# A graph-attention stack on one core: the end of the last block in another order, and another choice of score slots behind it

## The chip, the cores and the metric

The kernel runs on one core of one Trainium2 chip. The metric is the device time of one execution in microseconds (us), lower being better; the median of three runs is given. Profiles show one further execution, with the start and duration of every instruction on the core's engines: PE (matrix products), DVE and ACT (elementwise work on two engines of different instruction sets), POOL (a slower elementwise engine) and SP (which here only issues transfers). Each engine takes its instructions in the order in which they stand in its own queue.

## The reference

The input is `x` of shape (16, 1024, 128) and one 0/1 matrix `adj` of shape (1024, 1024). Three transformer layers with masked attention (8 heads of 16) are followed by one graph-attention layer:

```python
# layers 0, 1, 2
Q, K, V = (h @ Wq, h @ Wk, h @ Wv)            # split in 8 heads of 16
scores = einsum('bnhd,bmhd->bhnm', Q, K) / sqrt(16)
attn = softmax(where(adj == 0, -inf, scores))
x = layer_norm(h + (attn @ V) @ Wo + bo)
x = layer_norm(x + relu(x @ W1 + b1) @ W2 + b2)
# layer 3
h = x @ W;  s_i = h @ a_src;  s_j = h @ a_dst
e = leaky_relu(s_i[:, :, None] + s_j[:, None, :], 0.2)
att = nan_to_num(softmax(where(adj == 0, -inf, e)))
out = layer_norm(att @ h + x)
```

All is float32.

## The kernel before, in words

The work of a layer of one batch is a *block*: 48 blocks, m = 0 to 47, from 3 layers times 16 batches. Batches go in groups of four, so the last four blocks, 44 to 47, are layer 2 of the batches 12, 13, 14 and 15. A block has 32 *steps*, one for each of two groups of four heads, two halves of 512 queries and eight tiles of 128 keys. A step (`score_step`) makes four 128x512 tiles of exponentials (one for each head): PE writes scores into one of three PSUM *score slots* of 1,024 float32 (tag `s`, `slot()`), DVE or POOL puts the mask on, ACT takes the exponential. In five steps of eight ACT reads the scores first and POOL multiplies by the 0/1 mask (`L430`, about 2.15 us); the rest is masked by an addition on DVE (`L432`). Four steps later (`AHEAD`) `av_step` multiplies the exponentials by the values into one accumulator (`L449`). When the eight steps of a half are done, `finish` takes the accumulator out.

All other work is cut into *pieces*, small functions that put their instructions into the queues when called. There are chains of pieces:

- `proj_tasks`: the eight pieces of the next block's projections;
- `post_tasks`: for blocks 0 to 46 the eleven pieces behind a block's attention (gather, two of the output projection, two transposes, four of the first and two of the second feed-forward product); for block 47 the same work in two chains of six, one for each half of the queries (*final* 0 and 1), where half 0 can begin after step 19;
- `last_tasks`: for a batch whose layer 2 is done, the twelve pieces of layer 3, called the *last chain* below: two transposes (`xt`), three of `nodes`, `rows_gh`, then `edges(0)`, `edges(1)` with `aggregate(0)`, `edges(2)` with `aggregate(1)`, `edges(3)` with `aggregate(2)`, `aggregate(3)` and `end`. `rows_gh` turns columns into rows and issues 16 small transfers; `edges` (`L606`, `L609`) makes masked weights through two score slots, `aggregate` (`L296`, 128 matrix products) multiplies by them, and `end` normalises and stores.

The order is a plan made before anything runs. `now` counts steps. A piece is due at a fixed step of the block where the table `AT` names its chain (`proj` and `post`), or else so many steps after the piece before it in its chain. Behind each step `piece()` calls one due piece, of the first chain in the list that has one. In the block after a block of batch b, `AT["post"]` puts the last two pieces of `post_tasks(b)`, the two halves of the second feed-forward product, at steps 32 and 40, which is step 0 and step 8 of the block after that. The chain `last` follows in the same queue, its first piece five steps later.

After step 31 of block 47 come eight more turns (`for n in range(n, n + 2 * AHEAD)`), in which the last four `av_step`s and one piece each are called, and then the loop `while chains`, which goes on counting and calls every due piece of every chain. I call the time from the end of the last `av_step` on the *tail*.

PE and ACT get their instructions in the order of this plan (`tc.manual_schedule`). The order on DVE, POOL and SP is the framework's, which builds it from the same program. Pieces write their matrix products into `bank()`: one PSUM bank of 512 float32 with a single buffer (tag `t`), except at the head of the program (`head[0]`), where it is half of a score slot. A piece that needs the bank waits until the piece before has been read out of it.

The changed lines are in `bank`, `rows_gh`, `put`, `av_due` and the end of the plan's loop. In `rows_gh` four pairs of transfers for r = 0 go to SP; the four pairs for r = 1 go to the ACT queue for the batches 14 and 15, to SP otherwise.

Of the kernel before, what the change touches and what calls it, by code (L numbers as in the profile page):

```python
# [31 lines left out]


AT = {"proj": (3, 6, 9, 11, 14, 15, 19, 20), "post": (12, 22, 23, 25, 26, 27, 28, 30, 32, 40, 41)}
AHEAD = 4
BOTH_ON_DVE = (2, 5, 7)
TILES = {"w": 10, "x": LANES + 1, "last": 2}
# [77 lines left out]
def fast_path(ctx: ExitStack, tc: tile.TileContext, a: dict, out: bass.AP, flag):  # L115
    nc = tc.nc
    x_dram, adj = a["x"], a["adj"]
    B, N, D = x_dram.shape
    NT = N // P
# [9 lines left out]
    def slot(dtype=F32):  # L129

        return psum.tile([P, N], dtype, tag="s", name="s", bufs=3)

    def bank():

        if head[0]:
            return slot()[:, :512]
        return psum.tile([P, 512], F32, tag="t", name="t", bufs=1)

    head = [True]

    def half_tile(name):

# [81 lines left out]
    def first_weights():  # L224
        W[0].update(load_layer(nc, nc.sync, const, a, 0, ("Wo", "b2", "W1", "b1", "W2", "ln1_g", "ln2_g")))
        norm_weights(nc.sync, 0)
# [49 lines left out]
    def soon():  # L276

        return nullcontext() if head[0] else tc.high_priority(offset=SOON)
# [167 lines left out]
    def av_step(step, e, acc, first, last):  # L446
        m, g, qh, kt = step
        for j in range(J):
            nc.tensor.matmul(acc[j * SLOT:j * SLOT + HD + 1, :], v_bufs[m % 2][:, kt, 2 * j + g, :], e[:, j, :],  # L449
                             start=first, stop=last)  # L450
# [89 lines left out]
    def last_tasks(b):  # L540
# [39 lines left out]
        def rows_gh():  # L580
            ps = bank()[:2 * NT, :P]
            nc.tensor.transpose(ps, s["col"][:, 0:2, :].rearrange("p c t -> p (c t)"), identf)
            parts = work.tile([2 * NT, 2, P], F32R, tag="parts", name="parts", bufs=1)
            with soon():
                nc.scalar.copy(parts[:, 0, :], ps)
                nc.vector.tensor_sub(parts[:, 1, :], ps, parts[:, 0, :].bitcast(F32))  # L586
            for r in range(2):

                queue = nc.scalar if r and b >= B - 2 else nc.sync
                for i in range(4):  # L590
                    row = 64 * r + g0 + i
                    queue.dma_start(g_rows[row:row + 1, :].bitcast(F32), parts[:NT, i // 2, :].bitcast(F32))
                    queue.dma_start(h_rows[row:row + 1, :].bitcast(F32),
                                    parts[NT + 4 * r:NT + 4 * r + 4, i % 2, :].bitcast(F32))
# [59 lines left out]
    blocks = [(b, l) for p in range(0, B, LANES) for l in range(L) for b in range(p, p + LANES)]  # L654
    chains = []
    done = {("fetch", b) for b in range(2)}
    now = [0]
    free = dict(TILES)
    free["x"] -= 2

    def put(tasks, mark, chain=None, first=False):

        if chain is None:
            chain = {"due": now[0], "queue": deque()}
            chains.insert(0 if first else len(chains), chain)
        for n, task in enumerate(tasks):
            at = now[0] // (4 * NT) * 4 * NT + AT[mark[0]][n] if mark[0] in AT else None
            chain["queue"].append(task + (mark if n == len(tasks) - 1 else None, at))
        return chain

    def take(chain):

        _, f, tiles, mark, _ = chain["queue"][0]
        if any(free[t[1:]] == 0 for t in tiles.split() if t[0] == "+"):
            return False
        chain["queue"].popleft()
        f()
        for t in tiles.split():
            free[t[1:]] += -1 if t[0] == "+" else 1
        done.add(mark)  # L680
        chain["due"] = now[0]
        if not chain["queue"]:
            chains.remove(chain)
        return True

    def is_due(chain):
        gap, at = chain["queue"][0][0], chain["queue"][0][4]
        return now[0] >= (chain["due"] + gap if at is None else at)

    def piece():  # L690
        for chain in chains:
            if is_due(chain) and take(chain):
                return

    def need(mark):
        while mark not in done:
            first = next(c for c in chains if any(q[3] == mark for q in c["queue"]))
            assert take(first) or any(take(c) for c in list(chains) if c is not first)
# [27 lines left out]
    def av_due(n):  # L726

        for item in [w for w in waiting if w[2] <= n]:
            step, e, _ = item
            half = step[:3]  # L730
            if half not in accs:
                if accs:
                    continue
                accs[half] = sums
                left[half] = NT
            waiting.remove(item)
            left[half] -= 1
            av_step(step, e, accs[half], left[half] == NT - 1, left[half] == 0)
            if left[half]:
                continue  # L740
            m, g, qh = half
            b, l = blocks[m]
            while g == 0 and qh == 0 and last_attn:
                need(last_attn.pop())
            finish(g, qh, accs.pop(half))()
            if m == len(blocks) - 1:
                if g == G - 1:
                    if qh == 0:
                        final.append(post_tasks(b, l)[1])
                    put(final[0][qh], ("final", qh), first=True)  # L750
                    if qh == 1:
                        put(last_tasks(b), ("last", b), chains[0])
            elif g == G - 1 and qh == 1:
                post = post_tasks(b, l)[0]
                chain = put(post[:1], ("attn", b, l))
                put(post[1:], ("post", b, l), chain)
                last_attn.append(("attn", b, l))
                if l == L - 1:
                    put(last_tasks(b), ("last", b), chain)

    n = 0
    with tc.manual_schedule(engines={mybir.EngineType.PE, mybir.EngineType.Activation}):
        for m, (b, l) in enumerate(blocks):
            order = [(g, qh) for g in range(G) for qh in range(2)]
            if m in (0, len(blocks) - 1):
                order.sort(key=lambda x: x[1])
            for at, (g, qh, kt) in enumerate((g, qh, kt) for g, qh in order for kt in range(NT)):
                now[0] = n
                if at == (6 if m == 0 else 1):
                    stack(m, 1)  # L770
                if n == 6:
                    with tc.issue_after(behind["stack"]):
                        first_weights()
                        other_weights()
                if n == 20:
                    with tc.issue_after(behind["pool"]):
                        biases()
                if n == 40:
                    with tc.issue_after(behind["dve"]):
                        last_weights()  # L780
                if at == 0 and m + 2 < len(blocks) and blocks[m + 2][1] == 0:
                    put([(0, fetch(blocks[m + 2][0]), "+x")], ("fetch", blocks[m + 2][0]))
                if m + 1 < len(blocks):
                    if at == (6 if m == 0 else 0):
                        need(("post",) + (blocks[m + 1][0], blocks[m + 1][1] - 1) if blocks[m + 1][1] else
                             ("fetch", blocks[m + 1][0]))
                        put(proj_tasks(m + 1), ("proj", m + 1), first=True)
                    if at == (24 if m == 0 else 21):
                        need(("proj", m + 1))
                        stack(m + 1, 0)  # L790
                step = m, g, qh, kt
                if FIRST <= n < FIRST + 4:

                    with tc.manual_schedule(engines={mybir.EngineType.DVE}):
                        e = score_step(step)
                        neighbours(4 + n - FIRST)
                        masks(4 + n - FIRST, mask_rows(4 + n - FIRST))
                else:
                    e = score_step(step)
                waiting.append((step, e, n + AHEAD))  # L800
                av_due(n)
                piece()
                n += 1
        exponentials(0)
        for n in range(n, n + 2 * AHEAD):
            now[0] = n
            av_due(n)
            piece()
        while chains:
            now[0] += 1  # L810
            for chain in list(chains):
                if is_due(chain):
                    take(chain)
# [236 lines left out]
```

## Time and profile before

| | us |
|---|---|
| median of 3 runs | 4011.02 (4008.79 to 4011.72) |
| the profiled execution, span from first to last instruction | 4007.5 |
| block 45, step 0 to step 0 of the next (steps 3623.2 to 3696.4) | 73.2 |
| block 46 (3696.4 to 3773.0) | 76.6 |
| block 47 (3773.0 to 3874.2) | 101.2 |
| the last four `av_step`s (to 3884.3) | 10.1 |
| tail to the end of the span | 123.2 |
| PE busy, of the whole span | 3767.4 (94%) |
| DVE, ACT, POOL busy | 85%, 84%, 86% |

The starts of the blocks are those of their first score products (`L422`, four to a step). Times inside the span are us from its start. A row of the table of stretches gives the stretch, its length and the busy time of each engine in it with the number of instructions. `PEclk` is the share of its full clock that PE was granted. In the list of instructions the bracket at the end of a row is the time in which the engine stood idle before it, and what ended that.

### The profile page before, as it was taken

The page shows a single profiled execution, that of the slowest core. Times are in us where ns is not written, and L with a number is a line of the kernel's source. Part 1 is how long each engine was busy: PE and PEld are TensorE (multiplying, and loading weights), DVE is VectorE, ACT ScalarE, POOL GpSimd, SP SyncE. Part 2 cuts the span into 40 slices and gives each one's busy share as a digit, 9 for nine tenths or more (in the row PEclk, how much of TensorE's full clock was granted, in tenths as well). Part 3 has the DMA queues.
Part 4 walks back from the last instruction along what each step waited for, and adds up shares of the span by engine and source line. Part 5 has one row for each costly group of instructions (what it writes and reads, how often), then busy time and mean ns, then how long its engine had stood idle before and what let it go on. Part 6 is the DMA issues. An engine that isn't in the chain of part 4 may idle for free.

```text
span 4007.5 us, 107755 instructions
## 1 busy us (share of the span) xinstructions
PE 3767.4 (94%) x44501; PEld 1551.0 (39%) x44501; DVE 3412.3 (85%) x5326; ACT 3380.2 (84%) x3961; POOL 3450.1 (86%) x3010
## 2 busy tenths in 40 slices
PE   7999999999999999999999999999999999999986
PEld 2333333344443333334444333333444433333435
DVE  7888988988888988988888988988888898988864
ACT  7999999977779999997777999999777799999850
POOL 5889989988889989998788999989888899989884
PEclk8999999999999999999999999999999999999998
DMA  6222122212222222122222222222222121222100
GB/s 162 64 65 59 49 64 65 53 46 67 55 56 59 56 64 64 48 60 55 55 55 55 64 64 57 51 64 65 55 55 55 49 64 49 59 65 62 46 7 20
DMA packets 124465, 233.13 MB, mean 58 GB/s; under 512 B 34624, under 2 KB 73792, under 8 KB 123968
## 3 DMA queue, kind: packets, MB, share of 16 engines
q1 hardware_dynamic: 122960, 225.71, 22.5%
q8 instruction: 354, 5.80, 0.6%
q14 instruction: 143, 1.17, 0.1%
q10 hardware_dynamic: 1008, 0.44, 0.0%
HBM read 15.54 MB, written 8.39 MB: 6 GB/s over the span
## 4 chain that ended last, share of the span: by engine, by line
PE 60%; DVE 17%; POOL 16%; issue 4%; ACT 3%; SPq 1%; DMA 0%; ACTq 0%; DVEq 0%; POOLq 0%
PE acc L449 23%; PE t L296 19%; PE s L422 15%; DVE e L432 10%; POOL e L430 7%; POOL x L344 3%; POOL x L345 3%; DVE st L321 3%; PE t L285 2%; POOL mv L338 1%; DVE x L328 1%; ACT e L444 1%; DVE lo L385 1%; DVE mv L323 1%; POOL x L340 1%
## 5 line engine op out<-in xcount | busy, mean ns | idle before, releaser
L432 DVE TENSOR_TENSOR e<-s,mask_add 128x1024 f32<-128x1024 f32 x2112 | 2492.6, 1213 | 315.1 <-PE s L422 206.5
L444 ACT ACTIVATE e<-e 128x1024 f32<-128x1024 f32 x2112 | 2193.6, 1062 | 197.5 <-DVE e L432 181.6
L430 POOL TENSOR_TENSOR e<-e,mask 128x1024 f32<-128x1024 f32 x960 | 2052.9, 2152 | 343.4 <-ACT e L429 326.9
L449 PE MATMUL acc<-e,v 128*17 128x512 f32 x12288 | 1636.2, 604 | 61.9 <-POOL e L430 30.4
L422 PE MATMUL s<-Wq,Wk 64*128 64x512 f32 x6144 | 1177.0, 455 | 50.1 <-DVE e L432 33.6
L429 ACT ACTIVATE e<-s 128x1024 f32<-128x1024 f32 x960 | 982.9, 1024 | 245.9 <-PE s L422 245.8
L422 PEld LDWEIGHTS s<-Wq,Wk 64*128 64x128 f32 x6144 | 499.3, 186 | 1011.1 <-issue 397.5
L449 PEld LDWEIGHTS acc<-e,v 128*17 128x17 f32 x12288 | 208.0, 95 | 574.1 <-issue 466.9
L340 POOL TENSOR_SCALAR x<-x,mv 128x128 f32<-128x128 f32 x896 | 389.1, 448 | 23.5
L296 PE MATMUL t<-hd,e 128*32 128x129 f32 x8192 | 243.5, 276 | 5.7 <-DVE x L624 3.3
L338 POOL TENSOR_TENSOR mv<-mv,half_neg 128x4 f32<-128x4 f32 x224 | 232.5, 1038 | 18.6
L344 POOL TENSOR_TENSOR x<-x,ln_g 128x1024 f32<-128x1024 f32 (+1 forms) x97 | 229.6, 2367 | 10.3 <-PE t L285 6.3
L296 PEld LDWEIGHTS t<-hd,e 128*32 128x32 f32 x8192 | 226.3, 111 | 23.9 <-DVE lo L385 9.9
L328 DVE TENSOR_TENSOR x<-t,x 128x512 f32<-128x512 f32 x192 | 131.5, 685 | 93.5 <-PE t L296 93.5
L296 PE MATMUL t<-x1T,W 128*32 128x512 f32 x1536 | 200.1, 592 | 1.9 <-DVE x L624 1.0
L321 DVE BATCH_NORM_STATS2 st<-x 128x6 f32<-128x128 f32 x896 | 197.0, 279 | 3.3
L296 PEld LDWEIGHTS t<-W,hT 128*32 128x32 f32 x6144 | 174.0, 111 | 59.9 <-issue 45.5
L296 PE MATMUL t<-W,hT 128*32 128x128 f32 x6144 | 188.1, 275 | 1.8 <-ACT x1T L290 0.9
L285 PEld LDWEIGHTS t<-identf,x 128*128 128x128 f32 x888 | 95.8, 142 | 227.6 <-issue 87.5
L285 PE MATMUL t<-identf,x 128*128 128x128 f32 x888 | 156.0, 291 | 27.0 <-DVE parts L586 7.4
L385 DVE TENSOR_TENSOR lo<-t,hi 128x512 fp32r<-128x512 f32 x188 | 128.2, 682 | 35.6 <-ACT hi L384 35.6
L336 POOL TENSOR_SCALAR mv<-mv 128x4 f32<-128x4 f32 x224 | 53.0, 236 | 122.6 <-DVE mv L323 102.7
(97 smaller groups left out, 2507.7 us busy)
## 6 DMA issues: line engine op xcount, KB each, us to landing
Wk<-hi SPq DMA_DIRECT2D x384, 128.0 KB
Wk<-lo SPq DMA_DIRECT2D x384, 128.0 KB
Wq<-hi SPq DMA_DIRECT2D x384, 128.0 KB
Wq<-lo SPq DMA_DIRECT2D x384, 128.0 KB
x<-in_x_dram SPq DMA_DIRECT2D x16, 512.0 KB
out_dram<-x SPq DMA_DIRECT2D x31, 256.0 KB
ai<-in_adj_dram SPq DMA_DIRECT2D x8, 512.0 KB
g_rows<-parts SPq DMA_DIRECT2D x120, 4.0 KB
```

What stands on the lines that cost most here:

```text
L285: nc.tensor.transpose(ps[:, t * P:(t + 1) * P], src[:, 4 * h + t, :], identf)
L296: nc.tensor.matmul(dst[j:j + SLOT, :], lhsT[:, j:j + SLOT], rhs, start=start, stop=stop)
L321: nc.vector.bn_stats(st[:, t, :], z[:, t, :])
L338: nc.gpsimd.tensor_tensor(v, v, half_neg[:, ts], OP.pow)
L340: nc.gpsimd.tensor_scalar(z[:, t, :], z[:, t, :], mv[:, t, 0:1], mv[:, t, 1:2], op0=OP.add, op1=OP.mult)
L344: nc.gpsimd.tensor_mul(z, z, rows(gain, n))
L422: nc.tensor.matmul(ps[:, r * 512:(r + 1) * 512], k[64 * r:64 * r + 64, kt * P:(kt + 1) * P], q[64 * r:64 * r + 64, q0:q0 + 512], start=Tru ...
L429: nc.scalar.activation(ev, psv, AF.Exp, scale=HD ** -0.5)
L430: behind["pool"] = nc.gpsimd.tensor_mul(ev, ev, m).ins
L432: behind["dve"] = nc.vector.tensor_add(ev, psv, m).ins
L444: nc.scalar.activation(ev, ev, AF.Exp, scale=HD ** -0.5)
L449: nc.tensor.matmul(acc[j * SLOT:j * SLOT + HD + 1, :], v_bufs[m % 2][:, kt, 2 * j + g, :], e[:, j, :], start=first, stop=last)
```

## The change

The change does four things, all at the end of the program.

1. A second table, `AT_END`, gives other due steps to the ten timed `post` pieces of blocks 45 and 46 (`len(blocks) - m` is 3 and 2). For block 45 (batch 13) the two second feed-forward pieces are due at steps 30 and 31 of block 46. For block 46 (batch 14) all ten are due at steps 8 to 21 of block 47.
2. Since a `last` chain follows its `post` chain in the same queue, the last chains of batches 13 and 14 begin earlier too.
3. A flag `tail` is set where the loop `while chains` begins; from there on `bank()` is half of the next score slot, as at the head of the program, so all pieces and `edges` take the three slots in turn.
4. The r = 1 transfers of batch 14's `rows_gh` go to SP; only batch 15 keeps half of them on the ACT queue.

```diff
+AT_END = {3: (12, 21, 22, 24, 25, 26, 27, 28, 30, 31), 2: (8, 9, 13, 14, 15, 16, 17, 18, 20, 21)}
...
-        if head[0]:
+        if head[0] or tail[0]:
             return slot()[:, :512]
         return psum.tile([P, 512], F32, tag="t", name="t", bufs=1)
 
-    head = [True]
+    head, tail = [True], [False]
...
-                queue = nc.scalar if r and b >= B - 2 else nc.sync
+                queue = nc.scalar if r and b == B - 1 else nc.sync
...
-    def put(tasks, mark, chain=None, first=False):
+    def put(tasks, mark, chain=None, first=False, table=None):
...
-            at = now[0] // (4 * NT) * 4 * NT + AT[mark[0]][n] if mark[0] in AT else None
+            at = now[0] // (4 * NT) * 4 * NT + (table or AT[mark[0]])[n] if mark[0] in AT else None
...
-                put(post[1:], ("post", b, l), chain)
+                put(post[1:], ("post", b, l), chain, table=AT_END.get(len(blocks) - m))
...
+        tail[0] = True
         while chains:
```

## The prediction

> **What bounds the kernel now.** I read the stretches of time first, cut at the end of block 47's steps, the last product with the values (3884.3, which I call E), the first `edges` of batch 14 (3953.4) and the last aggregate.
>
> ```profile
> 3773.00:3874.20 101.20, 90.19 (x1307) 43.53 (x1303) 81.17 (x152) 65.00 (x79) 79.21 (x83) 0.93 0.11 28
> 3884.30:3953.40 69.10, 44.74 (x944) 34.47 (x941) 27.11 (x87) 8.38 (x26) 37.01 (x53) 0.79 0.04 11
> 3953.40:3995.10 41.70, 38.33 (x1093) 34.17 (x1089) 28.18 (x69) 0.65 (x4) 17.42 (x27) 0.93 0.06 17
> 3995.10:4007.50 12.40, 0.19 (x2) 0.11 (x2) 2.22 (x15) 0.00 (x0) 5.76 (x9) 0.70 0.17 49
> ```
>
> The first number after the length is PE. In block 47 it is busy 90.2 of 101.2 us, so a piece moved there is mostly paid there. In the first 69.1 us of the tail it is busy 44.7, partly at half clock: this stretch is waiting. Then come eight aggregates, bound by PE, and 12.4 us of closing work that the change leaves alone.
>
> The list of instructions tells who is waited for.
>
> ```profile
> 3839.43 8.39 POOL L430 TENSOR_TENSOR e<-e,mask 128x1024 f32<-128x1024 f32 x4
> 3841.62 1.91 PE L449 MATMUL acc<-e,v 128*17 128x512 f32 x8 [4.20 <-POOL e L430]
> 3849.20 1.30 PE L296 MATMUL t<-Wo,aT 128*32 128x128 f32 x32 [2.68 <-DVE aT L476]
> ...
> 3944.37 0.78 ACT L290 ACTIVATE xT<-t,ln_bc,ln_gc 128x512 f32<-128x512 f32 x1 [6.32 <-DMA g_rows<-parts]
> 3945.29 1.09 PE L285 MATMUL t<-identf,x 128*128 128x128 f32 x4 [5.94 <-ACT xT L290]
> ...
> 3967.36 3.75 PE L296 MATMUL t<-hd,e 128*32 128x129 f32 x128 [0.36 <-DVE x L624]
> 3991.30 3.75 PE L296 MATMUL t<-hd,e 128*32 128x129 f32 x128 [1.02 <-DVE x L624]
> ```
>
> In block 47 PE twice stands for POOL: four mask products are queued behind normalisations (4.20 us), and POOL's last step of a `finish` holds the next projection (2.68). In the tail ACT issues eight row transfers of batch 14 before it may evict batch 15's transpose, and PE stands 5.94 us. An aggregate is 3.75 us; the gap before it is 1.02, of which an `edges` (0.74) fills most where there is one.
>
> The chain that ended last shows the same: POOL until 3848, then PE and POOL in turn, ACT's queue at 3938 to 3944, then aggregates.
>
> ```profile
> 3839.48 8.34 POOL e L430 x4
> 3938.09 1.25 ACTq L592
> 3944.37 0.79 ACT xT L290
> 3956.32 5.20 PE t L296 x128
> 3962.58 3.79 PE t L296 x128
> ```
>
> **What the Trainium skill says.** "TensorE: Matmul & The Clock Gate", Part 1: an idle window of about 3.4 us puts PE at half clock until it has been busy for as long. The trace agrees: behind the 4.20 us wait a value product takes 1.91 us, not 1.05, and behind the 5.94 us wait an aggregate takes 5.21, not 3.75. "Perfetto Trace Analysis", Per-engine timelines: ACT, DVE and GpSimd are strict first-in first-out, PE pulls only weight loads ahead. The three waits above are such heads of queues. "Trainium Kernel Development and Optimization", Key Constraints: issuing transfers from several engines saves only issue time. In the trace that is much: batch 13's 16 transfers on SP take 3875.66 to 3886.37, 10.7 us, batch 15's 8 on SP beside 8 on ACT 6.2 (3955.25 to 3961.4).
>
> **Where the pieces go.** By the plan's rules with both tables, and by the queues of the two programs: from the tail (or the turns before it) to ahead of E come three `edges` and two aggregates of batch 13 and the two second feed-forward pieces of batch 14. Four first feed-forward pieces of batch 14 were ahead of E already. Left in the tail: half 1 of block 47, two aggregates of batch 13, and the last chains of 14 and 15. So the change does what it says. Batch 13's chain only gets half of its way, though.
>
> **Part 1: E.** PE work that comes in ahead of it: 3 x 0.74 + 2 x 3.75 + 2 x 1.93 = 13.6 us. What could hide it is the idle time of block 47, 11.0 us, of which the two POOL waits make 6.9 and half clock costs about 3.8 more. Does POOL's queue come out better? I set its new order against the PE pieces, with the durations of the trace: mask product 2.15, normalisation 3.3 (0.24 + 0.23 + 1.04 + 1.74 and small gaps), scale and shift 2.6 per half, 4.8 per whole. The old pile, a normalisation and 7.4 us of scaling ahead of four masks, is broken up. But the second normalisation behind batch 14's output projection now stands behind batch 12's last normalisation and scaling (5.9) and two masks (4.3), while its transpose is on PE already at step 19: the projection ends 52 us into the block, plus 2 for DVE; POOL reaches it at 61 and ends at 64.3; PE wants it at 59.6, so it stands 4.7 us. Two steps later the projection of half 0 waits about 2 us, as before, for a `finish` behind a mask product, and a transpose of the final chain 0.9. That is 7.6 where it was 6.9. I take no gain and E 13.6 later: about 3898. Bounds: 4 later if the stalls vanish (13.6 less 6.9 and most of the half clock), 19 if a new stall adds 5.
>
> **Part 2: E to batch 14's edges.** In before 69.1 us. In after, us from E, each from rows of before's tail:
> - the projection of half 1 starts at 2.7 (0.7 + 0.3 + 0.6 + 0.7 for transpose, reciprocal, POOL, transpose, and hand-overs) and ends at 3.8; DVE adds, and masks one half of batch 13's `edges(3)` first (1.2) before the statistics, to 7.0;
> - POOL meanwhile has batch 13's normalisation and scaling (5.9, from 1.9 to 7.8), then half 1's to 11.1;
> - transpose and ACT to 12.0, feed-forward 13.1, aggregate 3 of batch 13 16.9, feed-forward 17.9, nodes 18.8, second feed-forward 20.8, two more nodes 22.3, transpose and `rows_gh` 23.3, cast and difference 24.8;
> - SP has the second store of batch 13 ahead of these transfers: aggregate 3 (16.9) + DVE 2.0 + POOL 3.3 + 2.6, so 24.8 too. Transfers start at about 25.2;
> - all 16 on one queue: 10.7, and at most 1.7 until they can be used (batch 13: 3886.37 to 3888.06): 37.6. I add 1.5 for half clock in the chain: 39.
>
> PE is through batch 15's nodes at about 31 and waits for the transfers, with batch 15's `rows_gh` behind it. With half on ACT it would have been about 5 us less, but ACT would have been held. Saving: 69.1 - 39 = 30.1. Bounds: 37 if no half clock, 45 if half clock falls on the whole chain.
>
> **Part 3: aggregates.** In before 41.7, of which half clock is 1.5 (first aggregate) and about 1.2 (`edges`). Slots in turn do little: two for an `edges` and one for an aggregate is a period of three, so an aggregate gets the slot of the one before and waits as it did. The turn is broken where two `edges` follow one another: aggregate 2 of batch 14 gets the slot that batch 15's first mask pass reads, and waits for it, about 3.0 us more. Twice an aggregate follows another with no `edges` between; it takes another slot and saves 1.0. Net +1.0, the half clock kept: 42.7. Bounds 39 and 48. The closing 12.4 stays.
>
> The sum: 39 + 42.7 + 12.4 = 94.1 against 123.2, 29.1 less; E 13.6 later; net -15.5. The span goes from 4007.5 to 3992; the median of the runs stands 3.5 above the profiled span, so I forecast 4011.0 - 15.5 = 3995.5, say 3995. What a measurement can tell from no change is about 0.2%, 8 us: 4003 to 4019.
>
> **Rivals.**
> - *The likeliest*, paid in the block and earned twice over in the tail: 3995, own range 3987 to 4004. For it: PE idle 24 us in the first part of the tail. Chance 0.60, of which 0.05 lies within 0.2%.
> - *The block hides the work*: POOL's pile gone, no half clock, E only 4 later: 3986, down to 3979. For it: 11 us idle there. Against: POOL is as loaded as PE (79 + 5 us). Chance 0.21.
> - *The transfers take the gain*: SP is still on batch 13's store when rows are ready, 16 transfers in line, PE cold behind: batch 14's edges at 50 and not 39, aggregates 46; -15.5 + 11 + 3 gives 4009.5, no change. Against: the store's chain ends at 24.8 by the sum. Chance 0.11 (0.02 faster, 0.08 same, 0.01 slower).
> - *Slower*: the slots in turn bind. If each aggregate waited for the mask passes in its slot (2.4 us on DVE) as well as its own eviction, the eight aggregates cost 19 more; from -15.5 that is +3.5, 4014; with E 19 late instead of 13.6, 4020. It decides from 23.5 us over my sum, all eight aggregates with E at its late bound. Against: the slot order makes one pay. Chance 0.08.
>
> So faster 0.55 + 0.21 + 0.02 = 0.78, same 0.05 + 0.08 = 0.13, slower 0.09. The range 3979 to 4009 takes in the second rival and most of the third.
>
> **What would show it.** E near 3898 (3888 to 3904), block 47 some 107 us; a PE wait of 4 to 5 us before a transpose (`L286`) two thirds through it; 16 row transfers in a line on SP about 25 us behind E, and PE idle some 6 us before the `edges` that follow; one aggregate with a gap of 3 to 4 us before it, the others 1.0. I am wrong if E hardly moves, if the transfers aren't what batch 14's edges wait for, or if aggregates are more than 5.5 us apart.

## The result, and the profile after

The changed kernel takes 3994.27 us (median of 4 runs, 3992.41 to 3997.75), beside 4011.37 us for the kernel before on the same chip. The ratio is 0.9958, with a 95% interval of 0.9946 to 0.997: 17 us faster. The profiled execution has a span of 3990.6 us, where before it was 4007.5.

First the stretches of time of the changed kernel, cut at the same events as before: block 47's steps, the last four value products, E to the first `edges` of batch 14, the aggregates, the closing. Columns: stretch, length, busy time of PE, PEld, DVE, ACT and POOL with the number of instructions, granted clock, DMA share, GB/s.

```profile
3773.90:3876.70 102.80, 91.14 (x1289) 43.42 (x1285) 82.38 (x154) 67.90 (x83) 86.19 (x90) 0.97 0.09 25
3876.70:3894.20 17.50, 17.33 (x444) 12.40 (x440) 12.67 (x35) 3.87 (x5) 7.90 (x15) 1.00 0.01 3
3894.20:3933.50 39.30, 24.96 (x529) 20.01 (x527) 14.36 (x55) 7.65 (x28) 30.93 (x40) 0.79 0.06 17
3933.50:3978.20 44.70, 40.21 (x1088) 36.08 (x1088) 27.83 (x68) 0.26 (x1) 16.33 (x27) 0.88 0.06 16
3978.20:3990.60 12.40, 0.22 (x5) 0.11 (x2) 2.22 (x15) 0.00 (x0) 6.86 (x10) 0.65 0.17 49
```

The moved work is hardly seen in block 47, which is only 1.6 us longer than before, but in the line after it: the last value products take 17.5 us instead of 10.1, and PE is busy in 17.33 of them. (Block 46, which takes in one second feed-forward piece of batch 13, is 1.8 us longer.) E moves to 3894.2. From E to batch 14's edges there are 39.3 us where there were 69.1. The aggregates take 3 us more, the closing is the same.

The list of instructions of the changed kernel shows the waits; the bracket is the idle time before an instruction and what ended it.

```profile
3841.19 1.77 PE L286 MATMUL t<-identf,x 128*128 128x128 f32 x4 [4.58 <-POOL x L341]
3849.00 1.08 PE L297 MATMUL t<-Wo,aT 128*32 128x128 f32 x32 [1.56 <-DVE aT L477]
3897.06 1.93 PE L297 MATMUL t<-Wo,aT 128*32 128x128 f32 x32 [2.84 <-DVE aT L477]
3902.51 19.04 SPq L639 DMA_DIRECT2D out_dram<-x  x2
3923.50 1.77 PE L286 MATMUL s<-identf,x 128*128 128x128 f32 x4 [4.52 <-POOL x L341]
3933.53 1.19 PE L607 MATMUL s<-g_rows,h_rows 4*128 4x256 f32 x7 [4.97 <-DMA h_rows<-parts]
3944.06 3.75 PE L297 MATMUL s<-hd,e 128*32 128x129 f32 x128 [0.45 <-DVE x L625]
3951.52 5.28 PE L297 MATMUL s<-hd,e 128*32 128x129 f32 x128 [0.69 <-DVE e L610]
```

In block 47 the two waits for POOL of before (4.20 and 2.68 us) have become one of 4.58 at another place, the transpose of batch 14, and one of 1.56. In the tail PE no longer stands for ACT, but for the input of half 1's projection (2.84), for POOL (4.52) and for the row transfers (4.97). The last two lines are aggregates 1 and 2 of batch 14: 3.7 us lie between the end of the one and the start of the other, where others with an `edges` between them are 1.0 to 1.1 apart.

The chain that ended last, of the changed kernel (start, length, engine and what it works on):

```profile
3841.19 1.79 PE t L286 x4
...
3919.88 1.27 POOL x L346
3921.17 0.38 SPq L639
3921.64 0.65 SPq L593
...
3931.73 1.67 DMA h_rows<-parts
...
3937.53 5.46 PE s L297 x128
```

It runs through POOL's last operation on batch 13's output into the store of that output on SP, from there through the 16 row transfers of batch 14 in one line, and then into the aggregates.

### The profile page after: what moved, and what is told of

Read it like the earlier page. It is cut to its first block, busy times and chain, and to the rows that moved or that the text cites. A ratio compares the mean times of both kernels' runs of the same rounds, so it can differ in the third digit from the quotient of the medians.

```text
span 3990.6 us, 107765 instructions
## 1 busy us (share of the span) xinstructions
PE 3758.4 (94%) x44501; PEld 1550.6 (39%) x44501; DVE 3410.8 (85%) x5326; ACT 3380.6 (85%) x3961; POOL 3454.8 (87%) x3010
## 4 chain that ended last, share of the span: by engine, by line
PE 60%; DVE 18%; POOL 14%; issue 4%; ACT 3%; SPq 0%; DMA 0%; DVEq 0%; POOLq 0%; ACTq 0%
PE acc L450 23%; PE t L297 18%; PE s L423 15%; DVE e L433 10%; POOL e L431 7%; POOL x L345 3%; POOL x L346 3%; DVE st L322 3%; PE t L286 2%; DVE x L329 1%; POOL mv L339 1%; ACT e L445 1%; DVE lo L386 1%; PE s L297 1%; DVE mv L324 1%
## 5 line engine op out<-in xcount | busy, mean ns | idle before, releaser
L341 POOL TENSOR_SCALAR x<-x,mv 128x128 f32<-128x128 f32 x896 | 392.0, 453 | 23.5
L345 POOL TENSOR_TENSOR x<-x,ln_g 128x1024 f32<-128x1024 f32 (+1 forms) x97 | 230.0, 2372 | 11.7 <-PE t L286 6.1
L297 PE MATMUL t<-hd,e 128*32 128x129 f32 x7040 | 207.8, 275 | 1.2
L297 PEld LDWEIGHTS t<-hd,e 128*32 128x32 f32 x7040 | 193.5, 110 | 16.7 <-DVE lo L386 9.9
L610 DVE SCALAR_TENSOR_TENSOR e<-s,mask 128x1024 f32<-128x1024 f32 x128 | 150.3, 1213 | 6.1 <-PE s L607 5.4
```

What stands on the lines that cost most here:

```text
L297: nc.tensor.matmul(dst[j:j + SLOT, :], lhsT[:, j:j + SLOT], rhs, start=start, stop=stop)
L341: nc.gpsimd.tensor_scalar(z[:, t, :], z[:, t, :], mv[:, t, 0:1], mv[:, t, 1:2], op0=OP.add, op1=OP.mult)
L345: nc.gpsimd.tensor_mul(z, z, rows(gain, n))
```

## The experiments

Blocks ahead of the change differ by up to 9 us from profile to profile (block 46 begins at 3692.8 to 3701.6), so I count every profile from the first score product of block 46. *E* is then the length from there to E; the next columns are the stretches behind it. A profile is one execution, and the runs of one kernel scatter by some 5 us either way (28 runs of before on one chip: 4005.7 to 4016.06): where the time lies is read from the profile, the worth of a kernel from the ratio. The ratio is to runs of the kernel before on the same chip. e1 to e4, e5 to e8 and e9 to e12 ran on three different chips, with medians for before of 4011.19, 4009.13 and 4011.16 us, so medians of different groups are compared only roughly.

| kernel | flag | table | row queue of batch 14 | E | E to edges | aggregates | closing | sum | median us | ratio to before |
|---|---|---|---|---|---|---|---|---|---|---|
| before | | | ACT+SP | 187.9 | 69.1 | 41.6 | 12.5 | 311.1 | 4009.13 to 4011.37 | 1 |
| the change | x | x | SP | 198.7 | 39.3 | 44.7 | 12.4 | 295.1 | 3994.27 | 0.9958 (0.9946 to 0.997) |
| e1 | | x | ACT+SP | 198.6 | 54.0 | 45.7 | 12.6 | 311.0 | 4008.78 | 0.9998 (0.9989 to 1.0006) |
| e2 | x | x | ACT+SP | 198.7 | 34.5 | 43.1 | 12.6 | 288.9 | 3987.54 | 0.9942 (0.9929 to 0.9956) |
| e3 | | x | SP | 198.6 | 50.3 | 46.1 | 12.4 | 307.4 | 4011.19 | 1.0002 (0.9994 to 1.0011) |
| e4 | x | | SP | 188.0 | 59.9 | 42.0 | 12.3 | 302.3 | 4002.5 | 0.998 (0.9973 to 0.9987) |
| e5 | x | | ACT+SP | 187.9 | 54.8 | 41.0 | 12.6 | 296.3 | 3996.54 | 0.9973 (0.9961 to 0.9985) |
| e6: late transpose | x | other | SP | 203.7 | 50.8 | 44.8 | 12.2 | 311.5 | 4010.7 | 1.0002 (0.9994 to 1.001) |
| e7: own banks | x | x | SP | 198.7 | 39.4 | 42.3 | 12.7 | 293.1 | 3992.63 | 0.9957 (0.9943 to 0.9971) |
| e8: store on POOL | x | | ACT+SP | 188.0 | 49.9 | 41.7 | 12.5 | 292.1 | 3989.86 | 0.9955 (0.9941 to 0.9968) |
| e9: own banks | x | x | ACT+SP | 198.7 | 34.5 | 40.7 | 12.7 | 286.6 | 3983.36 | 0.9935 (0.9922 to 0.9949) |
| e10: e9, scaling on DVE | x | x | ACT+SP | 201.5 | 38.3 | 42.9 | 12.0 | 294.7 | 3990.82 | 0.9955 (0.9941 to 0.9968) |
| e11 | x | block 46 | ACT+SP | 193.3 | 47.2 | 47.4 | 12.3 | 300.2 | 3999.78 | 0.9973 (0.9962 to 0.9983) |
| e12 | x | block 45 | ACT+SP | 193.4 | 51.5 | 48.0 | 15.0 | 307.9 | 4007.0 | 0.9989 (0.9982 to 0.9996) |

My theory at the start was that of the prediction: the table moves work to where it costs less than it did, and the slots in turn do little.

**e1, the table alone.** The change without the flag, and with the queue line of before:

```diff
-        tail[0] = True
...
-                queue = nc.scalar if r and b == B - 1 else nc.sync
+                queue = nc.scalar if r and b >= B - 2 else nc.sync
```

> The table alone: no flag, and batch 14's r = 1 transfers on the ACT queue as before. Theory of moved work (the prediction's): the products with the values end at the same place as in the changed kernel (about 10 us later than before); in the tail the rows leave on two queues, 5 us earlier, and pieces share one bank, 2 to 4 us more; so 3990 to 3996, as fast as the changed kernel. Rival 'slots' (the flag brings the gain): 4005 or more. Rival 'ACT set free' (the queue line brings the gain): 4000 or more.

**e3, the change without the flag.**

```diff
-        tail[0] = True
```

> The changed kernel without the flag: behind the last attention step pieces keep the one bank. Theory of moved work: nodes and transposes wait for their bank to be read, about 3 us up to the rows, of which the store on SP hides some; the wait of 4.0 us before aggregate 2 of batch 14 shrinks to 1.0 and two gaps of 1.0 come back: 3993 to 3998, the same within what can be told. Rival 'slots': 4005 or more.

Both miss, and in the same way: they lie where the rival 'slots' had put them, and without the flag the change is worth nothing. e3 is at 4011.19 and not at 3993 to 3998. The list of instructions of e3 in the first part of the tail shows why (the bracket is the idle time before). Below it stand two lines of the kernel before and two of the changed kernel:

```profile
3907.86 0.63 PE L286 MATMUL t<-identf,x 128*128 128x128 f32 x4 [0.96 <-ACT xT L291]
3910.88 1.94 PE L297 MATMUL t<-x1T,W 128*32 128x512 f32 x8 [0.87 <-ACT xT L291]
...
3928.61 0.65 PE L297 MATMUL t<-w_nodes,xT 128*32 128x130 f32 x16 [1.11 <-DVE hd L575]
3930.07 0.66 PE L286 MATMUL t<-identf,x 128*128 128x128 f32 x4 [0.81 <-DVE hd L575]
```

```profile
3934.05 0.87 PE L296 MATMUL t<-w_nodes,xT 128*32 128x130 f32 x24 [1.02 <-DVE x L624]
3936.03 0.65 PE L296 MATMUL t<-w_nodes,xT 128*32 128x130 f32 x16 [1.10 <-DVE hd L574]
```

```profile
3913.11 1.04 PE L297 MATMUL s<-x1T,W 128*32 128x512 f32 x8
3913.97 0.85 PE L297 MATMUL s<-w_nodes,xT 128*32 128x130 f32 x24
```

With the one bank (`t<-`) nearly every piece waits until the piece before has been read out of it, 0.8 to 1.1 us each time; with the slots (`s<-`) pieces follow one another without a gap. Between E and batch 14's edges PE has 16 gaps of 0.3 to 1.3 us in e3, 14.7 us in all; in the changed kernel there are 3, of 2.0 us in all. Before it was 15 gaps with 14.1 us. That is the worth of the flag, 12.7 us of idle time here, and I had not priced it for any piece but the aggregates. "Perfetto Trace Analysis" of the Trainium skill, Optimizing Tensor Performance, says it in a sentence: "Independent matmul groups should rotate through different PSUM banks so the ACT/DVE evacuation of one overlaps the next group's matmuls". The runs agree: 14.7 us of such gaps with one bank, 2.0 with the slots.

**e5, the flag alone.** `tail` as in the change, the table not used, the queue line of before:

```diff
-                put(post[1:], ("post", b, l), chain, table=AT_END.get(len(blocks) - m))
+                put(post[1:], ("post", b, l), chain, table=None)
...
-                queue = nc.scalar if r and b == B - 1 else nc.sync
+                queue = nc.scalar if r and b >= B - 2 else nc.sync
```

> Only the slots in turn behind the last attention step; the table and the queue line as before. If moving the work is what shortens the stretch behind the last product with the values, this is near the run with flag and queue line but no table (4002.5), or up to 5 us below it, because eight of batch 14's sixteen row transfers leave on the other queue: 3997 to 4003. If the flag alone carries the gain of the whole change, 3993 to 3996. If flag and table only help together, 4008 to 4012.

3996.54 lies half a us below the first range and half a us above the second, so the number decides nothing between them, the less so as before itself is 2 us faster on this chip. In the profiles the flag alone takes 14.8 us of the sum (311.1 to 296.3) and the whole change 16.0; but e5's profile is of its fastest run. By the ratios, 0.9973 and 0.9958, the flag alone brings some 11 us of 17. What it does is plain in the profile: E to edges falls from 69.1 to 54.8, and the small gaps from 14.1 us to 1.0.

**e4, flag and queue line without the table, and e2, flag and table with the queue line of before.**

```diff
 # e4
-                put(post[1:], ("post", b, l), chain, table=AT_END.get(len(blocks) - m))
+                put(post[1:], ("post", b, l), chain, table=None)
 # e2
-                queue = nc.scalar if r and b == B - 1 else nc.sync
+                queue = nc.scalar if r and b >= B - 2 else nc.sync
```

> Flag and queue line without the table: all pieces where they were before. Theory of moved work: the products with the values end where they ended before (3884); the slots save 4 to 6 us of bank waits in the tail and the ACT wait of 6 us goes, but the rows of batch 14 then leave in one line on SP and are the last thing again; aggregates 2 us more: 4005 to 4014. Rivals 'slots' and 'ACT set free': 3996 or less.

> The changed kernel with the queue line undone: batch 14's r = 1 transfers on ACT again. Theory of moved work: the 16 transfers on SP are what batch 14's first edges wait for (4.97 us idle of PE), and ACT has nothing urgent then; edges start about 5 us earlier, 1 or 2 us less half clock: 3987 to 3990. Rival 'ACT set free': PE waits for ACT's transposes as before, 3998 to 4002.

e2 is a hit: the queue line of the change costs time. By the profiles it costs 6.2 us with flag and table (e2 to the change), 6.0 with the flag alone (e5 to e4), and 6.5 with banks of their own (e9 to e7). The intervals of the single ratios overlap in these pairs, but taken to the median of before on its own chip every run of e2 (0.9950 at most) lies below every run of the change (0.9953 at least), and every run of e9 (0.9943) below every run of e7 (0.9952); the margin is small, and the profiles show the same in all three pairs. Only without the flag, e1 to e3, is it the other way round in the profiles (311.0 to 307.4), and there the ratios do not differ: in e1 PE stands 5.90 us for ACT, held by its transfers, in e3 2.68 us for the rows. Why it costs, in the list of e2 around the edges:

```profile
3927.44 1.77 PE L286 MATMUL s<-identf,x 128*128 128x128 f32 x4 [4.50 <-POOL x L341]
3929.45 0.78 ACT L291 ACTIVATE xT<-s,ln_bc,ln_gc 128x512 f32<-128x512 f32 x1 [6.15 <-DMA g_rows<-parts]
3932.37 1.06 PE L607 MATMUL s<-g_rows,h_rows 4*128 4x256 f32 x8
```

ACT is in fact held by its eight transfers until 3929.4. But the transpose that it is to evict ends at 3929.21, because PE had stood 4.50 us for POOL before it. So the hold of ACT costs hardly anything (0.24 us), and PE finds the rows ready; with all 16 on SP it waits 4.97 us for them.

e4 at 4002.5 lies between the two ranges that I had given it: below the one for a flag that does little (4005 to 4014), above the one for its rivals (3996 or less). What holds it shows in its list:

```profile
3933.39 0.38 SPq L639 DMA_DIRECT2D out_dram<-x  x1
3937.63 0.55 PE L607 MATMUL s<-g_rows,h_rows 4*128 4x256 f32 x1 [12.26 <-DMA g_rows<-parts]
3942.93 1.19 PE L607 MATMUL s<-g_rows,h_rows 4*128 4x256 f32 x7 [4.75 <-DMA h_rows<-parts]
```

Four of the transfers of batch 14 are issued by 3925.9; then SP stands for 7.5 us before batch 13's second store, which waits for POOL, with the other twelve behind it. PE waits 17 us. So I formed another theory: with the flag there, what the table brings is to get this store out of the rows' way.

**e8, the flag alone with this store on another queue.** Beside the two edits of e5:

```diff
-                queue = nc.scalar if h and b == B - 1 else nc.sync
+                queue = nc.scalar if h and b == B - 1 else nc.gpsimd if h and b == B - 3 else nc.sync
```

> The flag alone, table and queue line as before, and batch 13's second output store issued by POOL instead of SP, so that batch 14's row transfers do not stand behind it on SP. If, given the flag, the table brings its gain by getting this store out of the way of the rows, this run is near the run with flag, table and the old queue line (3987.5): 3986 to 3992, and at least 5 us below the flag alone. If the gain of the table is the work that leaves the stretch behind the last product, it is within 2 us of the flag alone.

3989.86 is inside the first range. The wait for the rows in e5, `[4.80 <-DMA h_rows<-parts]`, is gone, and E to edges falls by that much, from 54.8 to 49.9. By the ratios e8 (0.9955) is as fast as the change (0.9958), without any of the moved work. But it isn't the whole of the table: what is left in e8 is ACT, held by its transfers while PE has nothing else.

```profile
3927.47 3.69 PE L297 MATMUL s<-w_nodes,xT 128*32 128x130 f32 x64 [6.36 <-ACT xT L291]
```

e5 and e2 differ by the table only, and now the account closes. Waits over 1.3 us between E and edges are 1.72, 1.53, 6.20 and 4.80 in e5, together 14.2; in e2 they are 2.84 and 4.50, together 7.3. 6.9 us of waits are gone, and PE is busy 13.4 us less (38.4 to 25.0); E to edges falls by their sum, 20.3 (54.8 to 34.5). E comes 10.8 later and the aggregates take 2.1 more: 7.4 us net in the profiles; by the ratios, 0.9973 and 0.9942, it is some 12. In before and e1, without the flag, the table removes hardly any wait (9.8 us of long ones to 8.7, 14.1 of short ones to 13.8): there it is 15.1 against 10.7 and 4.1 us, that is nothing.

**e11 and e12, half a table each.** With the flag and the queue line of before:

```diff
 # e11 (beside e2)
+AT_END = {2: (8, 9, 13, 14, 15, 16, 17, 18, 20, 21)}
 # e12 (beside e2)
+AT_END = {3: (12, 21, 22, 24, 25, 26, 27, 28, 30, 31)}
```

> Flag, the queue line of before, and of the table only block 46's row: batch 14's last post pieces move into block 47, batch 13's stay where they were. If what the table brings is the earlier start of batch 14's chain, this keeps it at a third of the cost: the last product with the values 3 to 4 us later than without a table, the stretch behind it 40 to 46 us, in all 3984 to 3990. If what it brings is that batch 13's output store gets out of the way of the rows, the store stays late here and the run is near the flag alone: 3994 to 3999.

> Flag, the queue line of before, and of the table only block 45's row: batch 13's chain moves ahead, batch 14's stays. If the earlier start of batch 14's chain is what the table brings, the pieces of batch 13 no longer lie in its waits and the stretch behind the last product with the values is 42 to 46 us, with that product 6 to 7 us later: 3990 to 3996. If the store of batch 13 is what it brings, 3986 to 3990.

Neither half brings anything beyond the flag. e11 (3999.78) has the ratio of the flag alone, e12 (4007.0) a worse one, with intervals that just touch. e11's time is near the second value that I gave for it, but not for its reason alone, and e12 is outside both ranges: neither the early chain nor the store explains the table by itself. Of e12 the list of PE, then a line of e11's:

```profile
3922.87 1.77 PE L286 MATMUL s<-identf,x 128*128 128x128 f32 x4 [10.91 <-POOL x L341]
3936.83 0.38 PE L583 MATMUL s<-identf,col 128*16 128x128 f32 x1 [6.98 <-ACT col L572]
3946.05 1.42 PE L607 MATMUL s<-g_rows,h_rows 4*128 4x256 f32 x12 [7.16 <-DMA h_rows<-parts]
```

```profile
3930.69 1.25 ACTq L593 DMA_DIRECT2D g_rows<-parts  x1
3939.88 1.42 PE L607 MATMUL s<-g_rows,h_rows 4*128 4x256 f32 x8 [4.80 <-DMA h_rows<-parts]
```

In e12 three `edges` and two aggregates of batch 13 are out of the tail and batch 14's chain is still in it: PE waits for POOL and for ACT with nothing to put in between, and the row transfers leave only at 3929.94, 43.7 us behind E. In e11 batch 14's chain is ahead, but batch 13's aggregates stand between its pieces, so its first row transfer leaves at 3930.69, 37.8 behind E; in e2 it is 25. The two halves shorten this chain only together. That is read from the traces; no run separates it further.

**e6, the late transpose.** The wait of 4.58 us in block 47 looked as if it could be had by asking later. The edit has the transpose due at step 21 and the pieces behind it at 22 to 27; the expectation names step 22.

```diff
-AT_END = {..., 2: (8, 9, 13, 14, 15, 16, 17, 18, 20, 21)}
+AT_END = {..., 2: (8, 9, 13, 21, 22, 23, 24, 25, 26, 27)}
```

> The changed kernel with the second transpose of batch 14's post chain due at step 22 of block 47 instead of 14 (its later pieces at 23 to 27), so that POOL has the rows ready before PE asks for them. If the wait of PE for POOL in the middle of block 47 (4.6 us, and the half clock behind it) costs the last block time, the last product with the values ends 4 to 8 us earlier and the run is at 3987 to 3991. If POOL's own work sets block 47 wherever PE waits for it, nothing changes: 3993 to 3996. If the pieces moved toward the end now wait for POOL in turn or one falls behind the last product, it is slower: 3996 to 4000.

It is 4010.7: worse than all three, and all of the gain is gone. First the list of PE in e6, then a stretch of it, in which the last three numbers are granted clock, DMA share and GB/s:

```profile
3847.62 1.93 PE L297 MATMUL t<-Wo,aT 128*32 128x128 f32 x32 [5.06 <-DVE aT L477]
3851.73 0.66 PE L286 MATMUL t<-identf,x 128*128 128x128 f32 x4
3860.43 1.76 PE L286 MATMUL t<-identf,x 128*128 128x128 f32 x4 [3.88 <-POOL x L341]
...
3937.20 1.76 PE L286 MATMUL s<-identf,x 128*128 128x128 f32 x4 [7.40 <-POOL x L341]
```

```profile
3862.00:3866.00 4.00, 4.00 (x21) 1.04 (x20) 1.23 (x1) 2.75 (x3) 3.92 (x3) 0.50 0.00 0
```

The moved transpose (3851.73) has no wait any more, but POOL's pile is where it was, and the next piece that needs POOL runs into it: the projection of half 0, whose input POOL finishes (5.06 where it was 1.56). Then the transpose of half 0 waits too (3.88), because the scaling of batch 14's whole tile, which the moved transpose sets free, now falls into the middle of that half's normalisation on POOL. PE works at half clock for 13.5 us of the block where in the change it is 4.3, and block 47 takes 5.5 us more. What was pushed back piles up on POOL behind E: PE waits for it for 5.20 and 7.40 us there, and batch 14's rows leave 38.9 us behind E instead of 27.4. Of the two places tried for this transpose, the one with the wait of 4.58 us was the cheaper.

**e7 and e9, banks of their own for the aggregates** (e7 is the change, e9 has the queue line of before as well). Line numbers of e9 and e10 are nine to eleven higher.

```diff
+    own = [0]
+    def agg_bank():
+        if not tail[0]:
+            return bank()
+        own[0] += 1
+        tag = ("t", "acc")[own[0] % 2]
+        return psum.tile([P, 512], F32, tag=tag, name=tag, bufs=1)
...
-                e, ps = s["e", u], bank()
+                e, ps = s["e", u], agg_bank()
```

> The changed kernel, but behind the last attention step the aggregates take two banks of their own (the piece's bank and the accumulator's) in turn, while all else goes on with the three slots. If the ring of three slots is what holds the aggregates back, the wait of 3.7 us before an aggregate of batch 14 falls to about 1 and the eight others lose up to 0.4 each: 3987 to 3991. If the masked weights on DVE are what an aggregate waits for, nothing changes: 3993 to 3996.

> The changed kernel with the queue line of before and, behind the last attention step, banks of their own for the aggregates. If both effects of the profiles add up (4.8 us in front of batch 14's edges, 1.5 to 2.5 us in the aggregates), 22 to 27 us below the kernel before: a ratio of 0.9933 to 0.9945. If the aggregates' gain is not there in the medians, as the run with the banks alone suggests, 0.9942 to 0.995.

```profile
3936.59 3.75 PE L306 MATMUL acc<-hd,e 128*32 128x129 f32 x128
3940.28 0.74 PE L616 MATMUL s<-g_rows,h_rows 4*128 4x256 f32 x12
3942.86 0.50 PE L616 MATMUL s<-g_rows,h_rows 4*128 4x256 f32 x4 [1.85 <-DVE e L619]
3943.29 5.41 PE L306 MATMUL t<-hd,e 128*32 128x129 f32 x128
3948.63 0.74 PE L616 MATMUL s<-g_rows,h_rows 4*128 4x256 f32 x8
3949.30 3.75 PE L306 MATMUL acc<-hd,e 128*32 128x129 f32 x128
```

In e9's list aggregate 2 of batch 14 begins 2.95 us behind the end of aggregate 1, where it was 3.7: the aggregate itself waits for nothing, but the `edges` ahead of it now stand 1.85 us for a slot. So the first outcome came only in its smaller part: the gap did not fall to 1, but the waits of 0.35 to 0.45 us ahead of the other aggregates are gone. The aggregates take 40.7 us instead of 43.1 (e2), 42.3 instead of 44.7 in e7. The medians do not tell e7 from the change (0.9957 and 0.9958), so the miss stands, though the profiles show the 2.4 us. e9 is at the low end of its first range and is the fastest version: 3983.36 us (3982.3 to 3988.12).

**e10, e9 with most of the elementwise work of the tail on DVE.** POOL is busy 29.3 of the 34.5 us between E and edges, so I took it off:

```diff
+            on = nc.vector if tail[0] else nc.gpsimd
-            nc.gpsimd.tensor_scalar(z[:, t, :], z[:, t, :], mv[:, t, 0:1], mv[:, t, 1:2], op0=OP.add, op1=OP.mult)
+            on.tensor_scalar(z[:, t, :], z[:, t, :], mv[:, t, 0:1], mv[:, t, 1:2], op0=OP.add, op1=OP.mult)
...
+        on = nc.vector if tail[0] else nc.gpsimd
-        nc.gpsimd.tensor_mul(z, z, rows(gain, n))
-        nc.gpsimd.tensor_add(z, z, rows(bias, n))
+        on.tensor_mul(z, z, rows(gain, n))
+        on.tensor_add(z, z, rows(bias, n))
```

> The run before (old queue line, own banks), and behind the last attention step the scalings of normalise and the products and sums of scale_shift go to DVE; POOL keeps only the small operations on mv. If POOL is what bounds the stretch between the last product with the values and batch 14's edges (it is busy 29 of 34.5 us there, and PE waits 4.5 us for it), this stretch falls by 4 to 7 us and the closing by 1 to 2: a ratio of 0.991 to 0.993. If the rows' transfers or PE's own work come next at once, the stretch falls by 2 at most and the ratio is 0.993 to 0.9945. If DVE is held up so that edges and aggregates wait, it is slower than the run before: above 0.9945.

The third outcome: 0.9955, and every run of it is slower than every run of e9. Part of it is in block 47, where the instructions are the same. The list of PE in e10 first, then a stretch of it with the clock:

```profile
3841.39 1.77 PE L295 MATMUL t<-identf,x 128*128 128x128 f32 x4 [4.56 <-POOL x L351]
```

```profile
3844.00:3848.00 4.00, 4.00 (x18) 0.81 (x20) 1.23 (x1) 2.92 (x3) 4.00 (x3) 0.50 0.02 4
```

The wait is as long as in the change (4.58), but here the half clock begins only when PE is at work again; in all PE works 16.7 us of the block at half clock, in three spells, and the block is 2.8 us longer. The rest is in the tail. Its chain, as above:

```profile
3899.62 1.75 POOL x L351 x4
3901.40 0.70 DVE x L356
3902.12 0.04 DVE x L357
...
3902.73 0.69 DVE x L338
...
3903.47 5.21 PE t L306 x124
```

The products and sums of batch 13's output (`L356`, `L357`), which nobody waits for, now stand in DVE's queue, wait there for POOL, and hold the addition behind them (`L338`), for which PE waits 2.55 us. On POOL they stood in nobody's way. They are shorter on DVE (0.69 us against 1.28 on POOL for 128x512), and the time is longer all the same. Beside them PE still stands for transposes in e10 (1.44 and 3.33 us): POOL's share of a normalisation is still in that chain.

## Why the prediction was right, point by point

| step | predicted | measured |
|---|---|---|
| E later | +13.6 | +10.8 |
| E to batch 14's edges | 69.1 to 39 | 69.1 to 39.3 |
| aggregates | +1.0 | +3.1 |
| closing | 0 | -0.1 |
| sum | -15.5 | -16.0 |

A further 0.9 us is in the blocks ahead of the change. That the sum is right to half a us is in part luck: E came 2.8 us earlier than forecast and the aggregates cost 2.1 us more, and the two nearly cancel. The reasons given are only partly right.

- **Part 1, where the pieces go and POOL's queue.** The order set against PE's pieces by hand gave a stand of 4.7 us before the second transpose of batch 14; it is 4.58. The projection two steps later was to wait about 2 us and waits 1.56. e6 supports the reading that these waits are POOL's backlog and not a piece at the wrong place.
- **Part 1, "I take no gain" and 13.6 us of work.** E came 10.8 us later. The work was a little larger than listed: with busy time at half clock counted half, PE does 15.1 us more from block 46 to E than before (166.1 to 181.2). One first feed-forward piece of batch 14, which I had put ahead of E, starts only at 3884.27 in the kernel before, and its 1.06 us came on top. The larger miss was half clock, which I put at about 3.8 us in block 47 and took nothing off for. PE works at half clock for 11.7 us of block 47 before, in three spells, which costs about half of it, 5.9; after for 4.3, in one spell of 6.8, of which it was idle for the rest. That is 3.7 us less, and PE's idle time fell by 0.6: 15.1 - 3.7 - 0.6 = 10.8.
- **Part 1, the stalls and half clock.** I had said that the stalls stay as long and so does the half clock; the stalls nearly did, the half clock did not. "TensorE: Matmul & The Clock Gate" of the Trainium skill, Part 1, speaks of a free-running window of activity, and the switches of the clock in these profiles agree with that (last section). In the change the half clock begins inside the stall, and 2.5 us of it fall on idle time; in e10, with the same stall, it begins when PE is at work again, and E is 2.8 us later than in e9. The other six profiles with the whole table have E at 198.6 or 198.7.
- **"Block 47 some 107 us"** was wrong: it is 102.8. Pieces that the plan gives to the end of the block run in the four turns behind it, which take 17.5 us instead of 10.1. E is the same for it.
- **Part 2** is right to 0.3 us, since its chain was worked out for the changed program, with no wait for a bank in it. What failed is a sentence of Part 3, "Slots in turn do little", and with it the account of what causes the gain. I weighed the flag for the aggregates alone. For the some twenty pieces between E and edges it is the larger part: without it the same chain takes 50.3 us (e3), and what the table saves there is no more than what it costs.
- **Part 2, SP's queue.** The store of batch 13 and the rows were both put at 24.8 us behind E. The parts are ready at about 25.8, and SP's transfers begin at 27.4, behind the store: 1.6 us lost, a small piece of the third rival. The half clock put down with 1.5 us is in that chain: one aggregate of batch 13 took 5.40 us and not 3.75. The rest of that rival (edges at 50) did not come.
- **"With half on ACT it would have been about 5 us less, but ACT would have been held."** The first half is right (e2: 4.8), the second named a hold without asking who waits for it. With the flag PE's transpose was late for POOL anyway; without it (e1) PE does stand 5.90 us for ACT.
- **Part 3.** One aggregate pays for the ring, as said: 3.7 us lie between aggregates 1 and 2 of batch 14. (The starts of the aggregates are 5.3 us apart on the mean, but two of the seven distances, 6.6 and 7.5, are over the 5.5 that I had named as a sign of being wrong.) Two aggregates that follow another save 1.0 each, as said. What I had not counted is half clock behind that gap: aggregate 2 took 5.28 us and not 3.75. e7 and e9 put the worth of the ring at 2.4 us.
- **The rivals.** The block hiding the work put E only 4 us later, and it was 10.8. The slots as a cause for a slower kernel would have had to cost 23.5 us; e7 and e9 put the ring at 2.4.

What stays open: the medians put the flag at 17 us (e3 to the change) where the profiles show 12.3; e3's profiled execution was its fastest run, and where its slower runs lose time is not known. e12's closing is 15.0 us, with POOL busy for 9.8 of it (before: 5.8); why is not known. And why two halves of the table lose what the whole one gains is read from two traces, not tried by itself.

## What to carry to other kernels

When independent small pieces on PE share one PSUM bank, count them: here each cost a hand-over of 0.8 to 1.1 us where PE had no other work to lay over it, 14 us in all. Before moving a piece or an operation because an engine waits, ask what stands in the queue behind it in the new place, and who waits for that; a store, a row transfer and a product for an output each held up a chain here to which they did not belong. An edit that looks like the smaller part of a change should be run alone: here nothing was gained without the flag, the flag alone brought about two thirds of the gain by the ratios, and one line about queues took back more than a quarter of what the other two edits gave.

## What the runs showed that I had not expected

- Half clock keeps to a grid. In each of the fourteen profiles every switch of the granted clock, over all 4 ms, lies within 0.01 us of one grid of 3.413 us, and the grid lies elsewhere against the program in every execution. So spells are whole multiples of 3.41 us, but for a last one that the end cuts short: 3.41 or 6.83 in block 47, up to 23.9 in the tail (e1). At the same instruction, behind a stand of 4.6 us, half clock began 2.1 us into the stand in the changed kernel (3838.7 to 3845.5) and 4.8 us after its start in e10 (3841.6 to 3848.4).
- The idle window of the prediction need not be idle throughout. At full clock, half clock followed every 3.41 us of the grid in which PE was, by the profile, busy for less than 1.6 us, and some with up to 2.8. It began in e10 (3780.1) and in before (3781.7) where PE had stood less than a microsecond at a time.
- A row transfer of 2 or 4 KB takes 0.59 to 0.70 us of SP's queue where ACT issues none, and is there for PE 1.7 us behind its issue at the latest (the changed kernel). On ACT the first of batch 14's eight takes 1.25 us (before, e2), and when SP and ACT issue side by side, each takes 0.6 to 0.8.
- Scaling four 128x128 tiles in a row takes 1.11 us on DVE and 1.74 on POOL (`L351` in e10). The kernel with the faster operations was the slower one.
